# Local attention and whitening on one core: one softmax turned earlier, ScalarE copies given out later, one load put behind the first bands

## The chip, the cores and the metric

The kernel runs on one core of a Trainium2 chip. The metric is device time in microseconds; of the three runs before, the median is 734.1 us (733.29, 734.1, 739.12). Times inside a run are counted from the start of the profiled span. Engines are named as the profile names them: PE (TensorE matmuls), PEld (TensorE weight loads), DVE (VectorE), ACT (ScalarE), POOL (GpSimd), SP (SyncE). A small q behind a name is the engine's instruction queue, where DMAs are issued.

## The reference

Layer 0 turns `x` (4 images, 256 channels, 64x64) into 49 logits per pixel, takes a softmax over them and uses them as the weights of a dilated 7x7 neighbourhood. Layer 1 whitens the result over four groups of 64 channels.

```python
# layer 0: w1 is (128, 256, 7, 7), w2 is (49, 128, 1, 1)
k = lax.conv_general_dilated(x, w1, window_strides=(1, 1), padding=[(6, 6), (6, 6)], rhs_dilation=(2, 2), dimension_numbers=DN) + b1[None, :, None, None]
k = lax.conv_general_dilated(k, w2, window_strides=(1, 1), padding=[(0, 0), (0, 0)], dimension_numbers=DN) + b2[None, :, None, None]
attn = jax.nn.softmax(k, axis=1)
xp = jnp.pad(x, ((0, 0), (0, 0), (6, 6), (6, 6)))
shifts = jnp.stack([xp[:, :, 2 * u:2 * u + x.shape[2], 2 * v:2 * v + x.shape[3]] for u in range(7) for v in range(7)], axis=1)
x = jnp.einsum('bkchw,bkhw->bchw', shifts, attn)
# layer 1, g = 4 groups of nc = 64 channels, m = all pixels of all images
xc = x - mean
Sigma = EPS * I + jnp.einsum('gdm,gem->gde', xc, xc) / m
rTr = (1.0 / jnp.einsum('gii->g', Sigma))[:, None, None]
for _ in range(5):
    P3 = jnp.einsum('gij,gjk,gkl->gil', P, P, P)
    P = 1.5 * P - 0.5 * jnp.einsum('gij,gjk->gik', P3, Sigma * rTr)
out = jnp.einsum('gde,gem->gdm', P * jnp.sqrt(rTr), xc) * weight + bias
```

## The kernel before

**Convolution.** The two convolutions are folded into one from 256 channels to 49 logits. Because of the dilation by two, even and odd rows and columns do not mix: each image lies in SBUF as two tiles `slot`, one for each row parity, and there are five stores for the eight of them. The 7x7 convolution is done as a fast convolution: the rows of the input and of the weights are evaluated at seven points (`row_eval`, `ROWS`), then its columns (`col_ops`), the products are matmuls, and the logits are interpolated from them. For one row point, the seven column points are done in three banks: `BANKS = ((1, 2, 0), (3, 4, 6), (5,))`. The DVE makes the evaluated columns `xh` of the points 1, 2, 3, 4 and 5 from the evaluated rows `rb`. The points 0 and 6 (infinity) are plain copies of `rb`, and ACT makes these two: the "column copies" of the title, lines 541 and 547. `conv_bank` (line 573) issues the matmuls of one bank (line 599) and then the copy of the result out of PSUM by ACT into `pv` (lines 610 and 615, the "conv evictions"). `conv_step(k, i)` runs bank `i` of row `k`, and then `prepare(k + 1, i)`, which makes what the same bank of the next row needs.

**Attention.** `softmax` (first three images) or `softmax_rows` (last image) turns logits with PE transposes (line 998), so that pixels lie on partitions, takes the softmax over the 49 taps, and `move_terms` copies the 49 terms into a skewed tile `zt`. POOL writes it to a DRAM scratch `sd`, and `load_band` reads it back on SP as matrices `band` and `bandz` (`load_band`, the last lines before `blocks`). One unit of attention, numbered `n` (0 to 15, four to an image), has two halves. `first_half` and `second_half` transpose blocks of x on PE (`make_block`, L1216, copied to `xb` and `xbz` by ACT, or by the DVE near the end, L1230 and L1239), multiply them with the bands (`weighted_sum`, L1267), write y back over x (`store_y`, ACT on L1287 and, in the last stage, DVE on L1285), transpose y (`turn_y`, L1298, copied to `yt` by ACT on L1306), and sum the moments for the whitening (L1319). Transposes take turns in three PSUM tiles `tp`.

**Order.** Every engine works its own queue in order. A scheduler places the instructions of the program order, with priorities (`tc.high_priority`), and `tc.add_manual_dep` can put one instruction behind another. While images 1 to 3 are convolved, the work of the image before is planned into eight gaps per image (`plan`, `gap`), each between two banks. A list `later` already holds back a few small ACT copies until the eviction of bank 1 (`conv_bank`, `if i == 1`). After the last convolution, the rest of the attention runs alone, from a list `rest`: first the last units of image 2 (n = 9 to 11), then n = 12 to 15 of the last image. The last image's softmax is done in two parts, `soft_start(0, ...)` and `soft_start(1, ...)`, and each in two row halves (`softmax_rows`, L1059 to L986). Then come the whitening chain and the pass that applies it and stores `out`.

**Loads of x.** POOL issues the loads of x. Image 2's even rows (`load_x(4, 4, ...)`, store 4) are planned into gap 2 of image 1. Half of that store holds the logits of image 0 until its softmax has been turned. The reload of image 0's odd rows, `load_x(1, 1, ...)`, already stands behind the last DMA of the first unit's bands (`load_band`, last lines).

Of the kernel before, what the change touches and what calls it, by code (L numbers as in the profile page):

```python
# [23 lines left out]
INF = 6  # L24
# [8 lines left out]
def kernel(  # L33
# [29 lines left out]
    nc = tc.nc  # L63
# [94 lines left out]
    def load_x(s, k, queue):  # L158
        slots[k] = store[s]
        if k in ahead:  # L160
            return [queue.dma_start(store[s].rearrange("p c r w -> p (c r w)"), ahead[k])]
        return read_x(halves(store[s]), k, queue)
# [85 lines left out]
    for k, c0 in enumerate(range(0, P, CB)):  # L248
        n = min(CB, P - c0)
# [276 lines left out]
            madd(r[1], r[2], -2.0, r[1])  # L526
        return rb[{1: 2, 2: 0, 3: 0, 4: 1, 5: 2, 0: 2}[br]]

    def col_ops(src, i):

        X = src.rearrange("p q r c (b a two) -> p (q r c b) a two", a=4, two=2)
        X4 = [X[:, :, a] for a in range(4)]
        o = {b: xh[b].rearrange("p (e two) -> p e two", two=2) for b in ORDER}
        E, O = ct[:, :, 0:2], ct[:, :, 2:4]
        EO = ct.rearrange("p e (a two) -> p e a two", a=2)
        if i == 0:
            add(EO, X[:, :, 0:2], X[:, :, 2:4])
            yield
            add(o[1], E, O)
            sub(o[2], E, O)  # L540
            nc.scalar.copy(o[0], X4[0])
        elif i == 1:
            madd(EO, X[:, :, 2:4], 4.0, X[:, :, 0:2])
            yield
            madd(o[3], O, 2.0, E)
            madd(o[4], O, -2.0, E)
            nc.scalar.copy(o[INF], X4[3])
        else:
            madd(o[5], X4[0], 2.0, X4[1])
            yield  # L550
            madd(o[5], o[5], 2.0, X4[2])
            yield
            madd(o[5], o[5], 2.0, X4[3])

    def col_eval(src, i):
        for _ in col_ops(src, i):
            pass

    def both0(src, br, i):
# [8 lines left out]

    slot = {}

    later = []

    def conv_bank(b, br, i, w):

        if i == 0:
            slot[b, br] = len(slot) % NV if b == 0 else (len(slot) - NV) % 2
        pts = BANKS[i]
        i0 = sum(len(k) for k in BANKS[:i])
        cv = cv_buf[ncv[0] % 2][:, : 3 * PT].rearrange("p (n q f) -> p n q f", n=3, q=Q9)
        ncv[0] += 1  # L580
        if b == 0:
            xv = {bc: xh[bc].rearrange("p (q e f) -> p e q f", e=2 * NCC, q=Q8) for bc in pts}
        else:
            xv = {
                bc: xh[bc].rearrange("p (e g q f) -> p e q g f", e=2 * NCC, g=2, q=Q8)
                for bc in pts
            }
        for k, bc in enumerate(pts):
            terms = [(sr, sc, cc) for sc in taps(bc) for sr in taps(br) for cc in range(NCC)]
            wv = w[bc].rearrange("p c (a r k) -> p c r a k", r=len(taps(br)), a=NCC)  # L590
            for j, (sr, sc, cc) in enumerate(terms):
                for h in range(2):
                    o = cv[
                        h * HB : h * HB + KT, k, sr : sr + Q8, 2 * sc : 2 * (sc + Q8)
                    ]
                    if b > 0:
                        o = o.rearrange("p q (g f) -> p q g f", g=2)
                    pe(
                        nc.tensor.matmul(  # L599
                            o,  # L600
                            wv[:, sc, sr, cc],
                            xv[bc][:, h * NCC + cc],
                            start=(j == 0),
                            stop=(j == len(terms) - 1),
                            skip_group_check=True,
                        )
                    )
        with tc.high_priority():
            full_ = len(pts) - (INF in pts)
            nc.scalar.copy(  # L610
                pv[:K2, slot[b, br], i0 : i0 + full_].rearrange("p n q b -> p (n q b)"),
                cv[:K2, :full_].rearrange("p n q f -> p (n q f)"),
            )
            if INF in pts:
                last = nc.scalar.copy(
                    pv[:K2, slot[b, br], i0 + full_].rearrange("p q b -> p (q b)").rearrange(
                        "p (q f) -> p q f", q=Q9
                    )[:, :, : 2 * Q8],
                    cv[:K2, full_, :, : 2 * Q8],
                )  # L620
        if i == 1:

            while later:
                tc.add_manual_dep(
                    later.pop()().ins,
                    last.ins.name,
                    mybir.DependencyInfo(
                        mybir.DependencyClass.NoSync, mybir.DependencyReason.DATA
                    ),
                    reason="later",  # L630
                )
# [177 lines left out]
    rows += [(b, br) for b in range(1, B) for br in ROWS if b > 1 or br]  # L809
    cur, nxt = {}, {}  # L810

    def prepare(k, i):

        b, br = rows[k]
        w = weights(b, br, i)
        if i == 0:
            cur["x"] = row_eval(b, br)
        nxt.update(w)
        col_eval(cur["x"], i)

    def conv_step(k, i):
        w = {bc: nxt.pop(bc) for bc in BANKS[i]}
        b, br = rows[k]
        conv_bank(b, br, i, w)
        end = b > 0 and br == ROWS[-1]
        if end:

            with in_order():
                if i == len(BANKS) - 2:
                    col_interp(b, br, 0)  # L830
                elif i == len(BANKS) - 1:
                    col_interp(b, br, 1)
                    row_interp(b, 1)
        last = i == len(BANKS) - 1 and br == ROWS[-2]
        if k + 1 < len(rows):
            with tc.high_priority() if last else nullcontext():
                prepare(k + 1, i)
        if i == len(BANKS) - 1 and not end:
            with in_order() if last else nullcontext():
                col_interp(b, br)  # L840
                if last:
                    row_interp(b, 0)
# [47 lines left out]
    def behind(dmas, name):  # L890
        for dma in dmas:
            tc.add_manual_dep(
                dma.ins,
                name,
                mybir.DependencyInfo(mybir.DependencyClass.Sync, mybir.DependencyReason.DATA),
                reason="behind",
            )
# [173 lines left out]
        soft_done.add((b, pc, h))  # L1071

    terms, moved, loaded = {}, set(), set()
    written, soft_done, moved_by = [], set(), {}

    MOVES = [(0, 0, 4), (2, 0, 2), (2, 2, 2)]
    MOVES += [(s, j, 1) for s in (1, 3) for j in range(CR)]
# [83 lines left out]
    def load_band(n, half):  # L1161

        if (n, half) in loaded or n not in moved:
            return
        loaded.add((n, half))
        D = sd[n % 2][:]
        base = lambda t, h: (
            h * HS + TR8 * t * RS + (ROW0[t] - TR8 * t + R) * WS + COLS[h][0] - h * TC + R
        )
        t0 = 2 * half  # L1170
        for h in range(2):
            nc.sync.dma_start(
                band[:, t0 : t0 + 2, h].rearrange("p t r w -> p t (r w)"),
                bass.AP(
                    tensor=D.tensor,
                    offset=D.offset + base(t0, h),
                    ap=[[LS - 1, P], [base(t0 + 1, h) - base(t0, h), 2], [1, TROWS * WS]],
                ),
            )
        e = CR * half + (R if half else 0)  # L1180
        for h in range(2):
            c0, c1 = COLS[h]
            dma = nc.sync.dma_start(
                bandz[h * 64 : (h + 1) * 64, half, :, c0:c1],
                bass.AP(
                    tensor=D.tensor,
                    offset=D.offset + h * HS + (HALF - CR * half) * RS + e * WS + c0 - h * TC + R,
                    ap=[[LS - 1, 64], [WS, R], [1, c1 - c0]],
                ),
            )  # L1190
        if (n, half) == (4 * B - 1, 1):
            bring_back(dma)
        if (n, half) == (0, 1):
            behind(load_x(1, 1, nc.gpsimd), dma.ins.name)

    blocks = {}

# [158 lines left out]
        if n % 2:  # L1356
            move(n // 2)

    def first_half(n, end=None):
        last = open_n.pop() if open_n else None  # L1360

        def turn(i):
# [19 lines left out]
        block(PIECES[1][2])  # L1382
        weighted_sum(n, 0, 3)
        weighted_sum(n, 0, 4)
        if end is not None:
            end()
        move_terms(n + 1, store_y(n, 0))
        half_done.add(n)
        load_band(n + 1, 0)
# [43 lines left out]
    def plan(b, j, *what):  # L1433
        todo.setdefault((b + j // NPC, j % NPC), []).extend(what)
# [25 lines left out]
    for b in range(B - 1):  # L1460
        for j in range(2) if b else ():
            plan(b + 1, j, lambda b=b, j=j: soft(b, j))
    plan(1, 2, lambda: load_x(4, 4, nc.gpsimd))

    def gap(b, j):
        for f in todo.pop((b, j), ()):
# [61 lines left out]
    move_terms(n + 1)  # L1528
    rest[2]()
    finish()  # L1530
    for t8 in range(4):
        for h in range(2):
            if (n, (t8, h)) not in blocks:
                make_block(n, (t8, h))
    rest[3](lambda: soft_start(1, False))
    rest[4]()
    soft_rows(1, 1)
    for f in rest[5:]:
# [219 lines left out]
```

## Time and profile before

| | before |
|---|---|
| median of 3 runs | 734.1 us |
| the profiled execution itself | 738.35 us, of which span 736.3 us |
| mean granted TensorE clock | 0.974 |
| PE busy, weight loads busy | 686.7 us, 542.4 us |
| DVE busy, ACT busy, POOL busy | 588.3, 341.4, 131.4 us |
| DMA | 126.09 MB, mean 171 GB/s |

The stages by time in the trace: weights and image 0's convolution to about 180 us, the convolutions of images 1 to 3 with the attention in their gaps to about 572 us, the attention alone to about 669 us, the whitening chain to about 682 us, and the application and the stores to the end. In a line of the timeline, the first number is the start in us, the second the duration in us, then follow the engine, the line in the code, the operation, output and input tile with shapes, and the count; a bracket gives the idle time before it and what ended that. Groups of instructions are merged into one line where they follow each other.

### The profile page before, as it was taken

How to read it: one execution, taken by the hardware profiler on the slowest of the kernel's cores; microseconds unless marked ns; L12 is line 12 of the kernel's file. 1: busy time of each engine (PE TensorE's matmuls, PEld its weight loads, DVE VectorE, ACT ScalarE, POOL GpSimd, SP SyncE). 2: the span in 40 equal slices, each digit the busy share in tenths (PEclk: the TensorE clock that was granted, in tenths of full speed). 3: DMA queues.
4: the chain of work that ended last, by engine and by line, in shares of the span. 5: the costliest groups of instructions: out<-in, count | busy, mean ns of one | idle time of the engine just before them, and what ended most of it. 6: DMA issues, size and time to landing. Idle time of an engine off the chain costs nothing. (4 is left out here: it accounts for less than half of the span.)

```text
span 736.3 us, 19131 instructions
## 1 busy us (share of the span) xinstructions
PE 686.7 (93%) x7728; PEld 542.4 (74%) x7728; DVE 588.3 (80%) x1278; ACT 341.4 (46%) x954; POOL 131.4 (18%) x190
## 2 busy tenths in 40 slices
PE   6999999999898999889999999898999886997996
PEld 1449543478898988788999989898998876895231
DVE  3799998994796989999886899899959768235575
ACT  1424320133654655566555444726546533432564
POOL 0002526624231020011220200202202032200000
PEclk9999999999999999999999999999999999897899
DMA  8933999924795394125784840363633154463598
GB/s 326 231 113 105 244 384 209 229 67 93 210 236 147 117 291 164 59 72 154 232 257 114 280 152 2 95 175 72 167 101 78 45 127 93 107 227 161 226 363 325
DMA packets 78720, 126.09 MB, mean 171 GB/s; under 512 B 36471, under 2 KB 59112, under 8 KB 77480
## 3 DMA queue, kind: packets, MB, share of 16 engines
q1 hardware_dynamic: 60488, 64.84, 28.1%
q0 software_dynamic: 12096, 41.77, 22.0%
q10 hardware_dynamic: 6048, 18.27, 7.9%
q8 instruction: 61, 1.00, 0.6%
q14 instruction: 27, 0.22, 0.1%
HBM read 78.78 MB, written 52.36 MB: 178 GB/s over the span
## 5 line engine op out<-in xcount | busy, mean ns | idle before, releaser
L599 PE MATMUL cv<-xh,wr 128*49 128x128 f32 x4160 | 232.3, 274 | 0.0
L599 PEld LDWEIGHTS cv<-xh,wr 128*49 128x49 f32 x4160 | 227.3, 124 | 3.3 <-issue 1.5
L1135 POOL DMA_DIRECT2D sd<-zt x124 | 65.5, 534 | 345.8 <-ACT zt L1116 279.1
L1267 PE MATMUL y<-band,xb 128*128 128x209 f32 x480 | 105.4, 346 | 7.8 <-DVE xb L1230 4.1
L1267 PEld LDWEIGHTS y<-band,xb 128*128 128x128 f32 x480 | 81.7, 194 | 9.1 <-DVE xb L1230 4.3
L610 ACT COPY pv<-cv 113x486 f32<-113x486 f32 (+2 forms) x60 | 26.2, 437 | 94.0 <-PE cv L599 89.3
L1306 ACT COPY yt<-tp 128x256 f32<-128x256 f32 x128 | 45.3, 379 | 40.4 <-PE tp L1298 39.1
L1298 PE MATMUL tp<-ident,slot 128*128 128x128 f32 x256 | 52.3, 301 | 8.7 <-ACT yt L1306 3.9
L354 DVE SCALAR_TENSOR_TENSOR pv<-pv 113x162 f32<-113x162 f32 x176 | 53.2, 322 | 3.5 <-ACT pv L610 2.7
L1298 PEld LDWEIGHTS tp<-ident,slot 128*128 128x128 f32 x256 | 41.2, 204 | 16.6 <-ACT yt L1306 5.2
L1216 PE MATMUL tp<-ident,slot 128*128 128x128 f32 x256 | 50.1, 303 | 2.8 <-ACT xbz L1239 2.8
L1287 ACT ACTIVATE slot<-y,pivot 128x512 f32<-128x512 f32 x53 | 36.5, 736 | 25.8 <-PE y L1267 25.7
L1216 PEld LDWEIGHTS tp<-ident,slot 128*128 128x128 f32 x256 | 41.0, 205 | 6.6 <-ACT xbz L1239 3.9
L147 POOL DMA_DIRECT2D slot<-in_x_dram x20 | 33.9, 1696 | 62.7 <-issue 46.6
L354 DVE SCALAR_TENSOR_TENSOR xh<-ct 128x512 f32<-128x512 f32 x40 | 26.7, 692 | 20.1 <-PE cv L599 20.1
L1116 ACT COPY zt<-d 32x112 f32<-32x112 f32 (+2 forms) x132 | 38.2, 289 | 9.6 <-DVE d L986 6.1
L1230 ACT COPY xb<-tp 128x256 f32<-128x256 f32 x96 | 33.5, 375 | 13.8 <-PE tp L1216 13.0
L1319 PE MATMUL sig<-yt 128*64 128x65 f32 x1024 | 39.5, 233 | 0.0
L1319 PEld LDWEIGHTS sig<-yt 128*64 128x64 f32 x1024 | 34.8, 146 | 5.8 <-issue 4.4
L1041 ACT ACTIVATE d<-tp,mx 128x49 f32<-128x49 f32 x96 | 27.6, 340 | 20.1 <-DVE mx L1036 11.7
L764 PE MATMUL acc<-slot,tap 128*49 128x256 f32 (+7 forms) x224 | 34.7, 468 | 0.0
L764 PEld LDWEIGHTS acc<-slot,tap 128*49 128x49 f32 x224 | 16.2, 123 | 17.9 <-issue 15.5
(242 smaller groups left out, 1118.4 us busy)
## 6 DMA issues: line engine op xcount, KB each, us to landing
out_dram<-out SPq DMA_DIRECT2D x32, 512.0 KB, 3.7
band<-sd SPq DMA_DIRECT2D x64, 242.0 KB, 3.0
slot<-in_x_dram POOLq DMA_DIRECT2D x20, 512.0 KB, 7.3
sd<-zt POOLq DMA_DIRECT2D x124, 77.0 KB, 3.0
wr<-gd ACTq DMA_DIRECT2D x14, 588.0 KB, 4.6
wr<-gd ACTq DMA_DIRECT2D x14, 490.0 KB, 5.0
ahead<-in_x_dram POOLq DMA_DIRECT2D x12, 512.0 KB, 7.4
spill<-slot POOLq DMA_DIRECT2D x3, 2048.0 KB, 10.1
```

Source lines behind the costliest of these rows:

```text
L147: queue.dma_start(o[:, cc, h], src[:, :, pr, h * SW : (h + 1) * SW])
L354: return in_turn(STT(o, a, f, b, ALU.mult, ALU.add))
L599: nc.tensor.matmul(o, wv[:, sc, sr, cc], xv[bc][:, h * NCC + cc], start=(j == 0), stop=(j == len(terms) - 1), skip_group_check=True,)
L764: nc.tensor.matmul(ps[h * HB : h * HB + KT, :, o0:o1], w[v][:, cc], rhs, start=(j == 0 and k == 0), stop=(j == len(order) - 1), skip_group ...
L1116: ins = nc.scalar.copy(o, i)
L1135: dma = queue.dma_start(bass.AP(tensor=D.tensor, offset=D.offset + h * HS + g * RS, ap=[[LS, TC], [CR * RS, NCH], [1, KS * WS]],), zt[p0 : ...
L1216: nc.tensor.transpose(t[:, cc * P : (cc + 1) * P], tile_of(xt, cc, t8, h, pc), ident)
L1267: nc.tensor.matmul(ps[:, cc, q0 : q0 + nq, c0:c1], xb[:, cc * P : (cc + 1) * P], rhs, start=(k == 0), stop=(k == len(PIECES[half]) - 1), s ...
L1287: last = nc.scalar.activation(o, i, AF.Identity, bias=pivot[:, cc : cc + 1])
L1298: nc.tensor.transpose(t[:, cc * P : (cc + 1) * P], tile_of(yt, cc, i // 2, i % 2, pc), ident,)
L1306: return nc.scalar.copy(yb.rearrange("p a g c -> p (a g) c")[:, :, :GW], t[:, :C].rearrange("p (e c) -> p e c", c=GW),)
L1319: nc.tensor.matmul(sig[g * GW : (g + 1) * GW, cc], yb[:, cc, g, :GW], yb[:, cc, g], start=(count[0] == 0 and cc == 0), stop=(count[0] == 4 ...
```

## The change

Three edits, and no computation is added or left out.

1. The column copies of ACT are no longer given out where `col_ops` stands. `prepare` hands `col_ops` a list, `points`, and `conv_bank` empties it after its eviction copies, at high priority and with a manual dependency on the last of these. So the copy for point 0 of row k+1, formerly behind the eviction of bank 0 of row k, is given out behind that of bank 1, and the copy for infinity behind that of bank 2.
2. `soft_start(1, False)`, which turns the second part of the last image's logits and starts their softmax, moves from the end of n = 12's `first_half` to ahead of the blocks of n = 12. `move_terms(14)` is called right behind it, where it formerly came at the end of `second_half(12)`.
3. `load_x(4, 4, ...)` is put behind the last DMA of the first unit's bands, as `load_x(1, 1, ...)` was.

```diff
-    def col_ops(src, i):
+    def col_ops(src, i, put=lambda copy: copy()):
...
-            nc.scalar.copy(o[0], X4[0])
+            put(lambda: nc.scalar.copy(o[0], X4[0]))
...
-            nc.scalar.copy(o[INF], X4[3])
+            put(lambda: nc.scalar.copy(o[INF], X4[3]))
...
-    def col_eval(src, i):
-        for _ in col_ops(src, i):
+    def col_eval(src, i, *put):
+        for _ in col_ops(src, i, *put):
             pass
...
-    later = []
+    later, points = [], []
...
-            nc.scalar.copy(
+            last = nc.scalar.copy(
                 pv[:K2, slot[b, br], i0 : i0 + full_].rearrange("p n q b -> p (n q b)"),
...
-        if i == 1:
-
-            while later:
+        for waiting in (points, later) if i == 1 else (points,):
+            while waiting:
+                with tc.high_priority() if waiting is points else nullcontext():
+                    copied = waiting.pop()()
                 tc.add_manual_dep(
-                    later.pop()().ins,
+                    copied.ins,
                     last.ins.name,
...
-    def prepare(k, i):
+    def prepare(k, i, *put):
...
-        col_eval(cur["x"], i)
+        col_eval(cur["x"], i, *put)
...
             with tc.high_priority() if last else nullcontext():
-                prepare(k + 1, i)
+                prepare(k + 1, i, points.append)
...
-    written, soft_done, moved_by = [], set(), {}
+    written, soft_done, moved_by, first_band = [], set(), {}, []
...
         if (n, half) == (0, 1):
-            behind(load_x(1, 1, nc.gpsimd), dma.ins.name)
+            first_band.append(dma.ins.name)
+            behind(load_x(1, 1, nc.gpsimd), *first_band)
...
-    def first_half(n, end=None):
+    def first_half(n):
...
-        if end is not None:
-            end()
         move_terms(n + 1, store_y(n, 0))
...
-    plan(1, 2, lambda: load_x(4, 4, nc.gpsimd))
+
+    plan(1, 2, lambda: behind(load_x(4, 4, nc.gpsimd), *first_band))
...
     rest[2]()
     finish()
+    soft_start(1, False)
+    move_terms(n + 2)
     for t8 in range(4):
         for h in range(2):
             if (n, (t8, h)) not in blocks:
                 make_block(n, (t8, h))
-    rest[3](lambda: soft_start(1, False))
+    rest[3]()
     rest[4]()
     soft_rows(1, 1)
```

## The prediction

> **What bounds the kernel now.** First the page's busy times: PE is busy for 93% of the span and its weight loads for 74%, the DVE for 80%, ACT for 46%. So PE's idle time is what can be won, and the PE waits say how much there is.
>
> ```profile
> PE 686.7 (93%) x7728; PEld 542.4 (74%) x7728; DVE 588.3 (80%) x1278; ACT 341.4 (46%) x954; POOL 131.4 (18%) x190
> ```
> ```profile
> PE y L1267 <- ACT xbz L1239: 7.1, 11, 1.5
> PE tp L998 <- ACT xb L1230: 4.3, 2, 2.2
> PE y L1267 <- DVE xb L1230: 4.1, 1, 4.1
> PE tp L1298 <- ACT yt L1306: 3.9, 3, 2.9
> PE tp L1298 <- DVE slot L1285: 3.6, 5, 1.3
> PE y L1267 <- DMA band<-sd: 3.4, 2, 2.0
> ```
>
> Columns: who waited for whom, us in total, times, longest. All are waits of the attention work; no convolution matmul (L599) waits for its columns or weights. Then I went through the timeline at each of PE's holes. Three places matter. The largest hole is in the attention of the last image:
>
> ```profile
> 615.94 0.74 DVE L1285 TENSOR_SCALAR slot<-y,pivot 128x512 f32<-128x512 f32 x1
> 616.74 0.83 PE L1298 MATMUL tp<-ident,slot 128*128 128x128 f32 x3 [0.76 <-DVE slot L1285]
> ...
> 622.75 2.67 DVE L1128 COPY zt<-d 128x56 f32<-128x56 f32 x11
> ...
> 625.45 1.09 DVE L1230 COPY xb<-tp 128x256 f32<-128x256 f32 x3
> ...
> 625.93 1.76 PE L1267 MATMUL y<-band,xb 128*128 128x209 f32 x4 [4.14 <-DVE xb L1230]
> ```
>
> The DVE works from 608.5 to 626.5 without a break: softmax, shuffles and term copies stand ahead of `xb`, so PE waits 4.14 us. Before that the DVE had idled: 2.10 us up to 602.55 and 3.31 us up to 608.52, waiting for PE.
>
> The second hole is at 497, where a column copy waits at the head of ACT:
>
> ```profile
> 495.88 2.28 DVE L354 SCALAR_TENSOR_TENSOR rb<-rb,rb 128x2048 f32<-128x2048 f32 x1
> ...
> 498.19 0.66 ACT L541 COPY xh<-rb 128x512 f32<-128x512 f32 x1 [6.98 <-DVE rb L354]
> ...
> 498.76 0.42 ACT L610 COPY pv<-cv 113x324 f32<-113x324 f32 x1
> 499.08 0.65 ACT L1306 COPY yt<-tp 128x256 f32<-128x256 f32 x2
> ...
> 499.51 0.51 PE L1298 MATMUL tp<-ident,slot 128*128 128x128 f32 x2 [2.93 <-ACT yt L1306]
> ```
>
> The third is the first unit's band, while the x load holds the DMA engines:
>
> ```profile
> 180.29 3.39 POOL L147 DMA_DIRECT2D slot<-in_x_dram  x2 [1.39 <-PE tp L998]
> ```
> ```profile
> 194.15 0.95 PE L1267 MATMUL y<-band,xb 128*128 128x209 f32 x4 [2.03 <-DMA band<-sd]
> ```
>
> In the 2-us windows from 182 to 194 the DMA share is 0.98 to 1.10, and bands issued at 180.6 to 184.7 took 11.3 us in the median, against 3.0 us over the whole page.
>
> **What the Trainium skill says.** "TensorE: Matmul & The Clock Gate", Part 1, What's actually happening: an idle window of about 3.4 us halves the PE clock, and the window runs free of the kernel. The trace agrees: after the hole at 497 the granted clock is 0.50 from 500.6 to 504, after the one before 598 from 599.6 to 603, and after the 4.14 us hole until past 630. But the 2.03 us wait at 194 and 2.18 us at 471 drew none, so a drop is chance. "DMA: Bandwidth & Descriptors", Issuing engines are not separate DMA queues: DMAs of SP, ACT and POOL share 16 engines and interleave; the window shares above agree. "Perfetto Trace Analysis", Identifying the Most-Contended Engine: matmul occupancy says little of the distance to the roofline. Here it only locates waits.
>
> **Edit 2, the softmax turned earlier.** I followed the order of instructions in both built programs, with durations from the rows of before. Both agree up to 601.88, when the last moments of n = 11 end. *PE* now turns the logits there: 8 matmuls, 1.09 us at full clock, about 1.8 because the clock is at half until 603. The three-buffer transposes of the blocks follow, paced by `xb` copies (0.42) on the DVE, and end near 606.0 instead of 604.75. The first half's y ends near 609.35; before it was 608.01, plus the 1.1 us turn after it. *ACT* has both exps (0.53 each) ahead of y's first copy. *DVE* now has, ahead of its half of y (L1285): two maxima (0.62), sum (0.56), two subtractions (0.62), reciprocal (0.19), mask product (0.22), scaling (0.57), second sum (0.56) and three shuffles (1.25), all between 607.35 and 612.2 with short waits. So L1285 ends near 612.95, and PE, which reached that point at 609.73 before, goes on at 613.0: **a new hole of 3.6 us, 3.3 us lost so far**. Next on the DVE: the last shuffle (0.6), n = 14's term copies (11, 2.6), scaling (0.8), shuffles (1.7), five copies of n = 15 (1.15): 620.1. There the second half's L1285 runs, until 620.85; PE resumes at 620.9 instead of 616.74: 4.2 us lost. The second half's y, even at half clock after the hole, ends by 619.0, so that cover hides a drop here. After 620.9 only 6 term copies, in twos and fours, stand between the `xb` copies, 0.9 us at most together; PE runs through and ends its moments near 627.6. Before they ended at 630.42. **Gain 2.8 us.** Bounds: all 4.14 + 2.1 (half clock over 625.93 to 630.1) won against 3.3 lost, 3.7 with luck; a second drop of the clock after 620.9 costs 1.7, leaving 1.1. Moving n = 14's terms also moves eight POOL writes (4.31 us of issue) from 619.24 to about 616.4; POOL idles 14.91 us before them, and band buffers come free later than that, so nothing of it reaches PE.
>
> **Edit 1, the column copies.** 16 pairs of copies move (0.67 us each). The wait at 498.19 is for `rb`, which the DVE finishes at 498.16 and still will. What changes is what stands behind it: the eviction and two `yt` go ahead. PE then does the next turn, one weighted sum and one more block transpose (0.23 + 0.71 + 0.23), until it needs a transpose tile whose copy is behind the copy of the columns, near 499.7. So the hole shrinks from 2.93 to about 1.6, **gain 1.2**; 2.93 + 1.7 if hole and clock drop vanished, which I keep for the range. Gaps behind bank 0 lose a copy: holes at 380.45 (1.00) and 537.69 (0.85) end on `xbz` right behind one, **0.6 each**. At 228.74 (1.08) and 230.75 (0.79) ACT waits for weights from the DVE, not for the copy: 0.2. The holes at 272, 299, 303, 327, 471 and 571 have other causes (row copy, weights, term copies, logits) and stay. Price of the added order: behind bank 1 the copy stands 0.66 us earlier in the gap's ACT work, ahead of `xb` and `yt`, while the one for infinity leaves that gap: zero in sum. Without that cover it is 0.66 in each of nine gaps, 6 us; I keep a loss of 1 for a gap or two. The consumers are PE's third point of bank 0 or 1 of the next row, at least 5 us away (bank 2's 1.8, two points of bank 0's 5.3). Readers of `rb` hold the DVE's next row no longer than its own bank-2 columns (3 x 0.68) do. **Sum 2.6**, from -1 to 5.
>
> **Edit 3, the load.** Of its four 512 KB DMAs two sat on POOL at 145.5, two at 180.29. All now stand behind the bands, the reload `load_x(1, 1)` and n = 1's writes, in POOL's order. The bands lose 1 MB of company, some 4 to 5 us at the 213 to 309 GB/s of 180 to 184, and land by about 189, an estimate. PE then runs from 191.9 on ACT's copies (0.76 per block for `xb` and `xbz`) and reaches the last product at 195.6 instead of 197.51: **gain 1.9**, from 0.5 to 2.3. The DVE waits 3.93 us for PE at 200.59, so it follows. The reload starts near 190 instead of 195.74, n = 1's writes near 202; the load is issued about 206 to 215. There it meets n = 1's first bands, wanted at 222: issued near 209, worst landing of before 11.5 us, so 220.5; 1.5 us of cover. The load's own reader is at 294. In SP's order the first two bands of n = 2 slip behind five weight transfers, from 230.6 to about 248; they are wanted at 266, so even 11.5 us leaves 6.
>
> **Sum.** 2.8 + 2.6 + 1.9 = 7.3. The profiled execution took 738.35 (span 736.3 + 2.05), so it would take 731.05. It lies 4.25 above the median of the runs; taking the same 7.3 off 734.1 gives **726.8**.
>
> **Rivals.**
> *Holes and clock both vanish.* For it: nearly every drop follows a hole, and edit 1 removes the longest one outside the last image. Then 3.7 + 5 + 2.3 = 11: 723. Against: `rb` still ends at 498.16. Chance 0.2.
> *The tail only moves its hole.* The DVE's work between 600 and 626 is unchanged; if the new 3.6 us hole brings a half-clock stretch that outlasts the DVE's backlog, and 620.9 brings another, edit 2 gives 0 and edit 1 about 1.5: 730.7. Chance 0.2.
> *Slower.* One mechanism: y's addition on the DVE stands behind both halves of the softmax. PE's next transpose, and behind it everything up to the whitening, waits for it. Each us that it comes after 612.95 is lost on PE until the second addition, which waits in the same line. The old hole returns 6.2 us at most; against 4.5 from the other edits, the change is slower if PE reaches its moments later than 634.9, that is if the two additions together come 7.3 us later than I have them. Exps that make the DVE wait, as in 0.57, 0.30 and 0.40 us before, would have to be ten times as long. Price then 736, with a third of this case beyond 741. Chance 0.08.
> *It doesn't do what it says:* excluded, since the built orders show all three moves.
>
> **How the numbers follow.** My case has 0.52, centre 726.8. The range runs from 720.5 (the bounds 3.7, 5 and 2.3 and one clock drop of 1.7 avoided besides, with a little for the runs' spread) to 733.5 (0, -1 and 1.9), leaving out about 0.2. A change of 1% is about what a measurement of this kernel can tell from none; the line is at 726.8, on my forecast, so my case splits in half: faster 0.26 + 0.2 = 0.46, within 1% 0.26 + 0.2 + 0.05 = 0.51, slower by over 1% 0.03.
>
> **What would show it.** Edit 2: no 4 us wait for `xb` near 620, but a wait for L1285 of 3 to 4 us in n = 12's turn. Edit 1: evictions of bank 1 no longer behind a 7 us wait; a shorter wait near 490 for an ACT copy. Edit 3: no wait for `band` near 190. Wrong if the granted clock falls from 0.974, if PE waits for `band` near 220, or if new waits for `yt` or `xb` come up behind the column copies.

## The result and the profile after

The changed kernel takes 729.09 us (725.86 to 732.76, 13 runs), the kernel before beside it 735.56 us (733.29 to 739.12, 13 runs). The ratio is 0.9906 with a 95% interval of 0.9884 to 0.9927: 6.9 us less, between 5.4 and 8.5. The profiled execution took 729.09 us, of which the span is 727.2, at a mean granted clock of 0.982. Against the profiled execution of before that is 9.26 us less, 2.8 us more than the medians differ (6.47); how far the granted clock accounts for that comes below. A half-clock stretch is in this text a run of some microseconds in which the granted clock is 0.50.

In the changed kernel the lines of the attention stand two further down: L1267 is now L1269, L1285 L1287, L1298 L1300, L1230 L1232. First the busy times of the page, then the waits of PE (who for whom, us in total, times, longest):

```profile
PE 683.2 (94%) x7728; PEld 539.2 (74%) x7728; DVE 587.0 (81%) x1278; ACT 341.5 (47%) x954; POOL 131.2 (18%) x190
```
```profile
PE y L1269 <- ACT xbz L1241: 5.9, 13, 1.5
PE y L1269 <- DMA band<-sd: 4.8, 2, 3.7
PE tp L1300 <- DVE slot L1287: 4.7, 5, 1.3
PE tp L999 <- ACT xb L1232: 4.2, 2, 2.2
...
PE tp L1300 <- ACT yt L1308: 1.0, 2, 0.8
```

The wait of 4.1 us for the DVE's `xb` is gone, and the waits for `yt` went from 3.9 to 1.0 us. The waits for a DVE addition grew only from 3.6 to 4.7. But the waits for a band rose from 3.4 to 4.8 us, and the longest is now 3.7: the sum had nothing for that, since the working gave these bands 1.5 us of cover.

The timeline at the three places, in the order of time. The first unit's band comes in time, its last product starts at 195.54 where it was 197.51:

```profile
195.54 0.66 PE L1269 MATMUL y<-bandz,xbz 128*128 128x96 f32 x4 [0.30 <-issue]
...
207.88 5.06 POOL L147 DMA_DIRECT2D slot<-in_x_dram  x3 [0.24 <-issue]
210.73 0.37 SPq L1173 DMA_DIRECT2D band<-sd  x1
...
227.06 1.76 PE L1269 MATMUL y<-band,xb 128*128 128x209 f32 x4 [3.73 <-DMA band<-sd]
```

The moved load is issued 3 us ahead of n = 1's first bands, and PE waits 3.73 us for one of these. The windows (us, PE busy with its count, granted clock, DMA share, GB/s) show a DMA share of 1.08 while PE waits, and a clock of 0.57 after it:

```profile
222.00:226.00 4.00, 1.34 (x10) 1.00 1.08 273
226.00:230.00 4.00, 2.94 (x11) 0.57 1.03 291
```

So the 2.0 us are paid back: PE's next common point is at 252.74, and was at 252.81.

The hole at 497 is down from 2.93 to 0.49 us. The copy of the columns still waits for `rb`, but the eviction and two `yt` are ahead of it, and PE gets one turn further before it waits. First PE's start in this gap before, then the changed kernel:

```profile
494.90 0.74 PE L1298 MATMUL tp<-ident,slot 128*128 128x128 f32 x4
```
```profile
493.88 0.75 PE L1300 MATMUL tp<-ident,slot 128*128 128x128 f32 x4
494.00 0.43 ACT L610 COPY pv<-cv 113x324 f32<-113x324 f32 x1 [3.80 <-PE cv L599]
494.42 0.65 ACT L1308 COPY yt<-tp 128x256 f32<-128x256 f32 x2
...
495.83 0.68 ACT L541 COPY xh<-rb 128x512 f32<-128x512 f32 x1 [0.58 <-DVE rb L354]
...
497.23 0.51 PE L1300 MATMUL tp<-ident,slot 128*128 128x128 f32 x2 [0.49 <-ACT xbz L1241]
```

In n = 12 the two additions of the DVE stand behind the softmax, and PE waits for each, as the working had it, but for 1.07 and 1.28 us (ahead of the first it waits 0.80 us more, for ACT's half of the addition):

```profile
604.71 0.39 PE L1300 MATMUL tp<-ident,slot 128*128 128x128 f32 x1 [0.80 <-ACT slot L1289]
...
605.34 0.77 DVE L1287 TENSOR_SCALAR slot<-y,pivot 128x512 f32<-128x512 f32 x1
...
606.16 0.62 PE L1300 MATMUL tp<-ident,slot 128*128 128x128 f32 x3 [1.07 <-DVE slot L1287]
...
612.88 0.75 DVE L1287 TENSOR_SCALAR slot<-y,pivot 128x512 f32<-128x512 f32 x1
...
613.69 0.84 PE L1300 MATMUL tp<-ident,slot 128*128 128x128 f32 x3 [1.28 <-DVE slot L1287]
```

Where the pair of traces differs, from matching starts of PE work (after less before):

| work | before | after | difference |
|---|---|---|---|
| last product of the first unit | 197.51 | 195.54 | -1.97 |
| after the bands of n = 1 | 252.81 | 252.74 | -0.07 |
| product that waited 0.30 us for `xbz` in both | 347.28 | 345.53 | -1.75 |
| product behind the hole at 380 | 380.45 | 378.02 | -2.43 |
| turn at which the changed kernel waits 0.49 us near 497 (before: the one after the hole's) | 500.94 | 497.23 | -3.71 |
| product behind the hole at 537 | 537.69 | 532.56 | -5.13 |
| turn in n = 11 | 598.20 | 593.09 | -5.11 |
| moments of the first half of n = 13 | 635.57 | 626.12 | -9.45 |

Of these, the step at 347 is no edit's: before had a half-clock stretch from 326 to 330 and the changed kernel has none there. In all, before has five such stretches ahead of the whitening chain, the last of them (622 to 632) twice as long as the others; the changed kernel has three (226 to 230, 469 to 472, 595 to 599). The sizes below are therefore taken from the medians of single edits, and the traces are used to say where.

### The profile page after: what moved, and what is told of

It reads as the page before. It is cut to its first block, busy times and chain, and to the rows that moved or that the text cites. A ratio compares the mean times of both kernels' runs of the same rounds, so it can differ in the third digit from the quotient of the medians.

```text
span 727.2 us, 19139 instructions
## 1 busy us (share of the span) xinstructions
PE 683.2 (94%) x7728; PEld 539.2 (74%) x7728; DVE 587.0 (81%) x1278; ACT 341.5 (47%) x954; POOL 131.2 (18%) x190
## 4 chain that ended last, share of the span: by engine, by line
PE 58%; DVE 26%; ACT 6%; DMA 5%; issue 4%; SPq 1%; POOL 0%; ACTq 0%; DVEq 0%; POOLq 0%
PE cv L599 17%; PE cv L765 8%; PE acc L765 8%; PE y L1269 7%; PE tp L1701 4%; PE sig L1321 3%; PE tp L1300 3%; DMA band<-sd 3%; DVE zz L354 3%; DVE pv L354 3%; DVE xh L354 2%; PE tp L1218 2%; PE cv L253 2%; DVE d L987 2%; DVE ct L354 2%
## 5 line engine op out<-in xcount | busy, mean ns | idle before, releaser
L1269 PE MATMUL y<-band,xb 128*128 128x209 f32 x480 | 104.3, 344 | 5.1 <-DMA band<-sd 4.8
L1269 PEld LDWEIGHTS y<-band,xb 128*128 128x128 f32 x480 | 81.0, 192 | 6.3 <-DMA band<-sd 5.4
L1300 PE MATMUL tp<-ident,slot 128*128 128x128 f32 x256 | 52.2, 300 | 8.1 <-DVE slot L1287 4.7
L1300 PEld LDWEIGHTS tp<-ident,slot 128*128 128x128 f32 x256 | 41.2, 204 | 16.2 <-DVE slot L1287 5.7
L1232 ACT COPY xb<-tp 128x256 f32<-128x256 f32 x96 | 33.5, 376 | 13.1 <-PE tp L1218 12.5
L1321 PE MATMUL sig<-yt 128*64 128x65 f32 x1024 | 37.4, 226 | 0.0
L1321 PEld LDWEIGHTS sig<-yt 128*64 128x64 f32 x1024 | 32.9, 139 | 5.5 <-issue 3.8
```

The source lines that it names most:

```text
L1269: nc.tensor.matmul(ps[:, cc, q0 : q0 + nq, c0:c1], xb[:, cc * P : (cc + 1) * P], rhs, start=(k == 0), stop=(k == len(PIECES[half]) - 1), s ...
L1300: nc.tensor.transpose(t[:, cc * P : (cc + 1) * P], tile_of(yt, cc, i // 2, i % 2, pc), ident,)
L1321: nc.tensor.matmul(sig[g * GW : (g + 1) * GW, cc], yb[:, cc, g, :GW], yb[:, cc, g], start=(count[0] == 0 and cc == 0), stop=(count[0] == 4 ...
```

## The experiments

Each edit is given against the kernel before or after, as named. Ratios are to the kernel before, measured beside it.

**One edit at a time.** Three kernels, each the kernel before with one of the three edits. Their diffs are the parts of the diff shown above; the core of each, in the order copies, softmax, load:

```diff
-                prepare(k + 1, i)
+                prepare(k + 1, i, points.append)
```
```diff
+    soft_start(1, False)
+    move_terms(n + 2)
...
-    rest[3](lambda: soft_start(1, False))
+    rest[3]()
```
```diff
-    plan(1, 2, lambda: load_x(4, 4, nc.gpsimd))
+    plan(1, 2, lambda: behind(load_x(4, 4, nc.gpsimd), *first_band))
```

> Edit 1 alone on the kernel before. Theory (each edit acts at its own holes): the holes near 380 and 537 shrink by about 0.6 us each and the one near 497 by 2 to 2.4 us, so 3.2 us less, ratio 0.9957; the recorded prediction had 2.6 us, 0.9965. The 4.1 us wait for xb near 620 and the 2.0 us wait for band near 194 stay. Rival (the clock decides, holes do not matter): ratio 1.000 on average, with a scatter of about 1.7 us per drop.

> Edit 2 alone on the kernel before. Theory: the 4.1 us wait for xb near 620 goes, two waits for the addition on L1285 of 1.0 to 1.3 us are late next, and the half-clock stretch from 622 to 630 goes with the long wait: 4.5 us less, ratio 0.994. The recorded prediction: a new hole of 3.6 us and 2.8 us less, 0.996. Rival (the hole only moves): a wait of 3 us or more for L1285 and ratio 1.000.

> Edit 3 alone on the kernel before. Theory: the wait for band near 194 goes (2.0 us less up to 200), and one of about 3.7 us comes near 225, because all four parts of the load now run while the second unit's bands are fetched: nothing is left, ratio 0.999 to 1.001. The recorded prediction: no second wait, 1.9 us less, ratio 0.9974.

| kernel | median | ratio | interval | us less |
|---|---|---|---|---|
| column copies | 734.52 | 0.9977 | 0.9963 to 0.9992 | 1.7 (0.6 to 2.7) |
| softmax | 733.35 | 0.9953 | 0.9938 to 0.9968 | 3.5 (2.4 to 4.6) |
| load | 737.34 | 1.0005 | 0.9987 to 1.0023 | -0.4 (-1.7 to 1.0) |

The kernel before took 736.59 us beside them, so that 0.0023 of it is 1.7 us. The three sum to 4.8 us, and their intervals allow 2.8 to 6.8 together (root of the summed squares); the whole change has 5.4 to 8.5. Whether the edits help each other is not told by this. Of the sizes expected, the load's came true, the softmax's 4.5 us lies just inside its interval, and the copies' 3.2 us lies above it.

With the copies alone, the hole at 497 shrinks to 0.88 us and those at 380 and 537 to 0.32 and 0.30, while the 4.14 us wait for `xb` stays. A wait of 0.68 us, of the convolution for its weights at 485.45, was not in the profile of before. Edit 1 is not shown to be its cause: the load alone, without that edit, has one of 0.82 us at 487.76. With the softmax alone, the timeline of n = 12 is that of the whole change:

```profile
613.00 0.62 PE L1298 MATMUL tp<-ident,slot 128*128 128x128 f32 x3 [1.05 <-DVE slot L1285]
...
620.53 0.83 PE L1298 MATMUL tp<-ident,slot 128*128 128x128 f32 x3 [1.28 <-DVE slot L1285]
```

With the load alone, the trace gains its 2.1 us at 195.38 and loses more than that in one wait, longer than in the whole change:

```profile
195.38 0.66 PE L1268 MATMUL y<-bandz,xbz 128*128 128x96 f32 x4 [0.30 <-issue]
...
228.50 1.76 PE L1268 MATMUL y<-band,xb 128*128 128x209 f32 x4 [5.32 <-DMA band<-sd]
```

So the third edit gains nothing by itself, and the wait belongs to it.

**The load two gaps later.** The changed kernel, with the load behind the last DMA of n = 1's bands.

```diff
+        if (n, half) == (1, 1):
+            first_band[:] = [dma.ins.name]
...
-    plan(1, 2, lambda: behind(load_x(4, 4, nc.gpsimd), *first_band))
+    plan(1, 4, lambda: behind(load_x(4, 4, nc.gpsimd), *first_band))
```

> The changed kernel with the load of image 2's even rows behind the last DMA of the second unit's bands instead of the first's. Theory (the load collides with whatever bands are fetched beside it): no wait for band near 194 and none near 225, the load runs near 225 to 240 where the DMA engines had little to do; 2 to 4 us less than the changed kernel, ratio to the kernel before 0.986 to 0.988. Rival (the second unit's bands are late for another reason, such as the late writes of the terms): the wait near 225 stays and the ratio is that of the changed kernel, 0.991.

726.94 us (723.77 to 728.34), ratio 0.9867, interval 0.9836 to 0.9899. The same kernel, measured again:

> The kernel of load_second once more, beside the others of this call: 0.987, with an interval narrow enough to tell it from the changed kernel's 0.9906, if the 3.73 us wait near 227 is worth what it shows (3.7 us of 736 is 0.5%). Rival (the wait is paid back by slack later in image 1): no lower than 0.990.

727.78 us, ratio 0.9878, interval 0.9855 to 0.9901. In both the band's waits near 194 and 226 are gone, and no band wait appears where the load now lies (issued from 221.5 to 230.8 in the second of the two). The mean of the two ratios, 0.9873, is 0.0033 below the changed kernel's, 2.4 us, but the single intervals overlap at their ends. The time thus points to the theory and does not settle it; what settles that the wait is the load's is the trace of these runs and the next.

**Half of the load.** The changed kernel, with only two of the four parts behind the first bands; the other two stay early.

```diff
-    plan(1, 2, lambda: behind(load_x(4, 4, nc.gpsimd), *first_band))
+    plan(1, 2, lambda: behind(load_x(4, 4, nc.gpsimd)[:2], *first_band))
```

> The changed kernel, with only two of the load's four parts behind the first bands; the other two stay where they were before, near 145 us. So the first unit's bands meet no x load at 180 to 194, and n = 1's first bands meet 512 KB fewer... that is half of it, 1 MB for 2 MB. Theory (the wait near 227 is the company of the late parts on the 16 DMA engines): the wait falls from 3.73 us to between 0 and 1.5, the bands' landing from 14.4 us to about 8, there is still no wait near 194, and the ratio to the kernel before is about 0.988. Rival (the bands near 215 are late for n = 1's own writes and the reload, not for this load): the wait stays above 3 us and the ratio at 0.991.

727.61 us, ratio 0.9874, interval 0.9849 to 0.9899. Here the issue view (transfer, queue, count, size of one, median us from issue to landing) for 209 to 222 us decides. First the changed kernel, then this one, then the load two gaps later (second measurement):

```profile
slot<-in_x_dram POOLq DMA_DIRECT2D x4, 512.0 KB, 9.1
band<-sd SPq DMA_DIRECT2D x4, 242.0 KB, 14.4
```
```profile
band<-sd SPq DMA_DIRECT2D x4, 242.0 KB, 7.1
...
slot<-in_x_dram POOLq DMA_DIRECT2D x1, 512.0 KB, 8.8
```
```profile
band<-sd SPq DMA_DIRECT2D x4, 242.0 KB, 3.7
```

The window cuts the list: this kernel issues two parts, at 207.04. The same four bands at the same place land in 14.4 us beside four parts (14.0 with the load alone), in 7.1 beside two, and in 3.4 to 3.7 with none (the kernel before, and the load two gaps later, where the window holds just the start of it). There is no wait for a band near 194 or 227. The rival, in which these bands are late for n = 1's own writes, falls: those writes are in all three kernels, and in the changed kernel and in this one the four bands are issued at the same times, from 210.73 and from 210.55. Two parts are not the whole price at other places: the first unit's bands in the kernel before took 11.3 us beside two parts at 180, where reads of 686 and 588 KB were under way as well.

**Only the copies for point 0.** The kernel before with edit 1, but the copy for infinity given out where it was.

```diff
-            put(lambda: nc.scalar.copy(o[INF], X4[3]))
+            nc.scalar.copy(o[INF], X4[3])
```

> Edit 1 alone, and only for the copy of point 0 (from behind bank 0 to behind bank 1); the copies for infinity stay where they were before. Theory (the holes near 380, 498 and 537 end on ACT work queued behind point-0 copies): all three shrink as with all copies moved, to 0.3, 0.9 and 0.3 us, and the ratio is 0.9977, within 0.002. Rival (taking the infinity copies away from behind bank 1 is what frees ACT): bank 1's gap now holds two copies, new waits for yt or xb of 0.6 us come up in several gaps, and the ratio is 1.000 or more.

732.91 us, ratio 0.9949, interval 0.9927 to 0.9972. The holes at 380 and 537 are gone as expected (0.31 and 0.30), so they do belong to the copies for point 0. The one at 497 is still long:

```profile
324.94 0.73 PE L999 MATMUL tp<-ident,lgx 113*128 113x113 f32 x4 [1.07 <-ACT xb L1231]
...
467.54 0.73 PE L999 MATMUL tp<-ident,lgx 113*128 113x113 f32 x4 [1.22 <-ACT xb L1231]
...
496.41 0.50 PE L1299 MATMUL tp<-ident,slot 128*128 128x128 f32 x2 [2.50 <-ACT xbz L1240]
```

It is 2.50 us, but it ends at 496.41 where before it ended at 499.51. PE arrives 3.85 us earlier (it starts this gap at 491.05, before at 494.90), and waits for the same thing: the DVE's `rb`, ready at 495.00. Some 2.2 us of these come with two half-clock stretches of before, at 230 and at 326, that this profile does not have (the changed kernel has none at 326 either); 0.7 are the hole at 380, and two waits for bands near 340 take 1.0 back. Not expected were the other 2.0: the holes at 326 and 471, which I had put down to term copies and said would stay, are halved. In ACT's timeline before the first of them, four term copies stood ahead of y (kernel before, then this kernel):

```profile
323.60 1.17 ACT L1116 COPY zt<-d 128x56 f32<-128x56 f32 x4 [1.40 <-DVE d L986]
324.78 1.36 ACT L1287 ACTIVATE slot<-y,pivot 128x512 f32<-128x512 f32 x2
```
```profile
322.64 0.25 ACT L1117 COPY zt<-d 128x56 f32<-128x56 f32 x1 [1.38 <-DVE d L987]
322.80 1.39 ACT L1288 ACTIVATE slot<-y,pivot 128x512 f32<-128x512 f32 x2
```

The scheduler placed three of the four behind the write of y: 0.92 us of ACT work off PE's path, twice, and nobody wrote that. Whether it makes the version faster than all copies moved is left open by these ratios (0.9949 and 0.9977, not measured beside each other, intervals overlapping); the run "Both" below speaks against it.

**The additions on ACT.** The kernel with the load two gaps later, and in n = 12 the second 512 elements of y's addition on ACT instead of the DVE, as in the stages before the last.

```diff
-                if tail and cc:
+                if tail and cc and n != 4 * (B - 1):
```

> The changed kernel, with the load planned two gaps later as in the run load_second, and the second write of y of n = 12 (the addition, twice 512 elements) on ACT in place of the DVE. Theory (the waits of 1.07 and 1.28 us at 606 and 614 are the additions' place in the DVE's order, behind the softmax): both fall below 0.8 us and PE is 1 to 1.6 us further on at 620; the end is as much earlier, ratio 0.985 where load_second has 0.987. Rival (the DVE's backlog is what limits the stage, the additions are only where it shows): the waits come back as waits for xb or for a band before 640, and the time is within 0.5 us of load_second.

> The kernel of add_on_act once more, beside mix: ratio 0.986 by the theory that the additions' place on the DVE cost 1 to 1.6 us against load_second; 0.988 if the first interval (0.9836 to 0.9887) was lucky. Waits near 325 and 468 of 2 us.

726.39 us, ratio 0.9861 (0.9836 to 0.9887), and measured again 724.34 us, 0.9857 (0.9833 to 0.9881). In n = 12 PE's waits for the additions are gone, and a shorter chain is left:

```profile
599.03 0.39 PE L1302 MATMUL tp<-ident,slot 128*128 128x128 f32 x1 [0.81 <-ACT slot L1291]
...
607.16 0.51 PE L1302 MATMUL tp<-ident,slot 128*128 128x128 f32 x2 [1.17 <-DVE xb L1234]
```

From the last six transposes ahead of n = 12's first products to the moments of its second half PE takes 20.46 us in the changed kernel, 20.38 with half the load, and 19.31 here (19.73 in the first of the two measurements). So the place in the DVE's order cost 0.7 to 1.1 us, less than the 1 to 1.6 expected, because one wait comes back for `xb`: the rival had that part right. By the time alone, 0.986 beside 0.987, the two kernels are not told apart.

**Both.** The kernel of the last run, with the copies for infinity where they were before.

> The kernel of add_on_act, with the copies for infinity where they were before. Theory (in only_point0 the waits near 326 and 471 fell from 2.0 and 2.2 us to 1.1 and 1.2 because, with a copy for infinity in that gap's ACT order, three of the four term copies ahead of y come after it; and the wait near 497 is as long as PE is ahead of the DVE's rb, whichever copies are moved): the waits near 325 and 468 are 1.1 to 1.2 us again, the one near 495 is 2 us or more, PE is 0.5 to 1 us further on at 575 than with all copies moved, and the ratio is 0.984 where add_on_act has 0.986. Rival (only_point0's ratio of 0.9949, beside 0.9977 with all copies, is chance of the two calls): waits as in add_on_act, ratio 0.986 or more.

724.6 us, ratio 0.9855, interval 0.9832 to 0.9877: no different from the run beside it (0.9857). The waits at 323.53 and 465.70 are 1.09 and 1.56 us, against 1.97 and 2.18 there, so the placing is reproduced. But PE is not ahead behind it: two waits for bands of 0.75 and 0.64 us come at 337 and 339, and a half-clock stretch, which the other does not have, runs from about 302 to 305. The wait at 495 was 0.94 us where I expected 2 or more, since PE, delayed, came later.

## Why the prediction was right, and where it was not

The predicted time was 726.8 us in a range of 720.5 to 733.5; 729.09 lies in it, and the gain of 6.9 us meets the sum of 7.3. Part of the 2.3 us between the two times is the start: the three runs shown had a median of 734.1 us, 13 runs beside the changed kernel 735.56. The mechanisms of the first two edits were right and the third term failed. That the sum came so close is in part luck: singly, the edits bring 3.5, 1.7 and -0.4 us for the 2.8, 2.6 and 1.9 predicted, 4.8 in place of 7.3. What fills the gap to 6.9 is not shown; the intervals allow that it is noise.

**Edit 2: right in kind; 2.8 us was within what the runs allow (3.5, from 2.4 to 4.6).** No long wait for `xb` is left near 620, and PE waits for the addition in n = 12's turn, but for 1.05 and 1.28 us and not for 3 to 4: both holes were over-sized. (The DVE's work from 608.5 to 626.5, called unbroken in the prediction, had two pauses there of 0.30 and 0.40 us, which change nothing.) To compare with the steps of the prediction, the run with this edit alone is moved back by 1.52 us (moments of n = 11 at 601.40, before 599.88). The first addition then ends at 611.43, not 612.95. The third and fourth maxima start at 606.63 instead of 607.35, and from there to the addition it takes 4.03 us, not 4.85: the "short waits" counted do not exist (from 605.1 to 621.6, in its own time, the DVE has no idle time in this run), and the rows overlap (one of 0.56 us starts at 608.83, the next at 609.31), so that their durations add up to more than the time they take. PE resumes at 611.48, 1.75 us later than before rather than 3.3, and after the second addition at 619.01, 2.27 later rather than 4.2. Its moments end at 626.51 and not 627.6: in place 3.9 us of gain. That agrees with the medians within their interval.

**Edit 1: right in place; 2.6 us was predicted, 1.7 measured (0.6 to 2.7).** The holes at 380 and 537 gave 0.69 and 0.55 us in the changed kernel, 0.6 each predicted. The 0.2 us at 229 and 231 did not come (1.19 and 0.78 us with this edit alone, for 1.08 and 0.79). The hole at 497 was to keep about 1.6 us and kept 0.49, or 0.88 with this edit alone. That is not more gain than predicted: the hole's length depends on how far PE is ahead of the DVE there. Take as the lead the time from PE's first transpose of this gap to the end of the DVE's `rb`:

| kernel | lead | wait of PE | difference |
|---|---|---|---|
| before | 3.26 | 2.93 | 0.33 |
| softmax alone | 2.66 | 2.32 | 0.34 |
| load alone | 2.20 | 1.87 | 0.33 |
| changed kernel | 1.92 | 0.49 | 1.43 |
| copies alone | 2.32 | 0.88 | 1.44 |
| only the copies for point 0 | 3.95 | 2.50 | 1.45 |

The later kernels with edit 1 have 1.44 to 1.46, or no wait where the lead is shorter than that. So the edit takes 1.1 us off this hole whatever the lead is, as long as some hole is left; at the lead of before 1.8 us would have stayed, for 1.6 predicted. The rest of the shrinking is PE coming later; what delays it there fits in size, the half-clock stretch from 469 to 472 in the changed kernel and the wait for weights of 0.68 us in the run of this edit alone. That wait comes and goes between executions or variants (0.82 us with the load alone, 1.61 with half the load, 0.57 with the additions on ACT, none in the changed kernel).

**Edit 3: the step that failed.** "There it meets n = 1's first bands, wanted at 222: issued near 209, worst landing of before 11.5 us, so 220.5; 1.5 us of cover." The times of issue were right to within 2.5 us (207.9 to 217.4 for the load, from 210.7 for the bands) and the gain at the first unit was 2.0 us for 1.9. What failed is the bound: 11.5 us had been measured where two parts of the load lay beside the bands, and beside four the bands took 14.4 in the median. PE waited 3.73 us, 5.32 with this edit alone, and a half-clock stretch followed in the changed kernel. A worst case taken beside two parts bounds nothing beside four. The prediction named this wait as one that would make it wrong; it cost the third term, 1.9 us.

**The clock.** The Trainium skill's "TensorE: Matmul & The Clock Gate", Part 1, What's actually happening, was used to say that a drop is chance. For the short waits the traces agree: the same wait of 2.18 us ahead of `lgx` was followed by a drop in the changed kernel (0.50 from 470 to 472) and by none before. On the length of the wait they differ from the page, which speaks of an idle window of about 3.4 us: a wait of 2.18 us was followed by a drop here, and in the kernel before one of 2.93. The long waits are less a matter of chance. With the load alone, whose profile has the wait of 5.32 us and then a clock of 0.50 from 226 to 232, the median granted clock of 22 runs is 0.974, where 59 runs of the kernel before have 0.979; with the softmax alone, without the wait of 4.14 us, it is 0.982. What one stretch costs in n = 12 shows in two kernels that differ little there: 21.86 us with a clock of 0.60 in 602 to 606 (the load two gaps later), 20.38 without a stretch (half of the load), so 1.5 us.

The clock also tells why the two profiles differ by 2.8 us more than the medians. A straight line through those 59 runs gives 0.41 us for 0.001 of granted clock, an estimate. The profiled execution of before had 0.974, which is 0.005 under their median, some 2 us; that of the changed kernel had 0.982, just the median of its 13 runs.

**The rivals.** "The tail only moves its hole" is out: the edit to the tail alone is faster over its whole interval. "Slower" is out by the ratio: the additions came earlier than I had them, not 7.3 us later. "Holes and clock both vanish" is out for the changed kernel: it had 11 us less, and 5.4 to 8.5 were measured. The versions that keep the load off the bands come near it, with 9 to 10.7.

**A better version.** The changed kernel with the load two gaps later and n = 12's addition on ACT is the fastest of those measured twice: 0.9861 and 0.9857, some 10 us less than before and 3.5 less than the changed kernel. Its upper bounds (0.9887 and 0.9881) lie at the changed kernel's lower one (0.9884).

## What to carry to other kernels

When a transfer is moved off one deadline, write down which transfers with a deadline it will lie beside next, and size their landing by the bytes in company, not by the worst landing of a page in which the company was smaller. A wait that ends on an engine's queue should be priced from that engine's order alone, one row after the other; idle time put in between as caution can be larger than the effect. And when an edit gives a scheduler freedom, compare the order of the other engines too: here three copies changed sides by themselves, worth as much as a hole that was aimed at. Last, a hole where one engine waits for another gets shorter when the waiting engine merely comes later; compare it by the lead of the one over the other before the edit is credited.

## What was not expected of the hardware

Four bands of 242 KB landed in 3.4 to 3.7, in 7.1 and in 14.4 us with none, two and four 512 KB parts of x beside them, though the parts themselves landed in 8.3 us (two) and 9.1 us (four) there, and in 8.2 to 9.0 us where all four lay behind these bands. The large transfers lose little by this company and the bands much; the two are on different queues, POOL's and SP's. Which property of the bands does it was not tried.
